# Issuing a pairwise-product kernel's stores and later loads from GpSimd's queue, one packet per DMA engine and transfer

## The chip, the core and the metric

The kernel runs on one core of a Trainium2 chip. The metric is the device time of one execution in microseconds. Before the change three runs took 1284.17, 1285.41 and 1285.61 us; their median, 1285.41 us, is what the changed kernel is compared with.

## What is computed

```python
def _L0_rec_ref(x, W):                      # x [4096, 32, 64] f32, W [64, 64] f32
    vid = jnp.einsum('bfd,de->bfe', x, W)
    idx_i, idx_j = jnp.triu_indices(32, k=1)
    return x[:, idx_i, :] * vid[:, idx_j, :]      # [4096, 496, 64]
```

Each of 4096 rows holds 32 fields of 64 numbers. Every field is multiplied by one 64x64 matrix, and then, for each of the 496 pairs i < j, field i is multiplied number by number with the transformed field j. The input is 33.6 MB and the output 520.1 MB, so nearly all that moves between the core and its memory is output.

## The kernel before

The host lays the batch out so that partitions hold (half of the batch, number within the field): two halves of 64 numbers make 128 partitions. A *tile* is 128 batch rows of each half; there are 16 tiles. In SBUF there is one large tensor, `mem`, of 445 *units*; a unit is 128 numbers, 512 bytes, in each of the 128 partitions. A tile of input takes 32 units (one for a field); a pair's product takes one unit, so 16 x 496 = 7936 units of output go out.

**Inputs** lie at the top of `mem` in two groups, `GROUPS`: tiles 0 to 7, and from tile 8 on the other eight. Tile 0 comes by itself in two transfers of the smaller tensor `x0`. The rest of group 0 comes in three pieces (128, 70 and 26 units), and group 1 in three more (102, 128 and 26 units), which overwrite group 0 when it is used up. `load(g)` issues a group.

**TensorE** multiplies each tile by a 128x128 matrix `w2` that holds W twice on its diagonal, and leaves the result in PSUM (`vid`), half a tile at a time, in a loop of its own.

**VectorE** (DVE) makes the products: 270 `tensor_tensor` instructions on line 299, each of which reads one operand from `mem` and one from `vid` and writes to `mem`. All its work stands in program order.

**Stores.** The stream of 7936 product units is cut into 74 *slots* (`SLOTS`: length, home in `mem`, and places where an instruction is split). As soon as the last product of a slot is issued, `store(slot, last)` issues one DMA of that slot, `(p u) c -> p u c`: each partition writes one contiguous row of up to 128 units, 64 KB, to the output. Homes are reused all the time: a product that is written over an old slot waits for that slot's store. Everything runs in the order in which it is written; no scheduler reorders anything.

**Queues.** A `Queue` object remembers what its engine already knows, so that it waits only for what it does not know. `transfer` (line 194) allocates a semaphore `moved<n>`, issues the DMA and adds 16 to the semaphore on landing. Loads go out on SyncE's queue (SP). Stores go out on SP up to slot 45, and from slot 46 (`SECOND`) on ScalarE's queue (ACT). GpSimd (POOL) has only four small memsets at the start. Each queue is in order: an instruction that waits holds what stands behind it. The first store after each group's loads also waits for that group's second piece (`hold[-2]`). At the end SP waits for what has not been heard of (line 313).

The constructor of the program sets aside 512 bytes in each partition for descriptors that software writes (`dynamic_dma_scratch_size=512`); before the change nothing used them.

Of the kernel before, what the change touches and what calls it, by code (L numbers as in the profile page):

```python
# [38 lines left out]
]  # L39

SECOND = 46


PAD = 24
# [111 lines left out]
def place_of(t, fields):  # L158

    first = max(begin for begin, _ in GROUPS if begin <= t)  # L160
    return TOP - (t - first + 1) * fields


def ends(tiles):
    return [begin for begin, _ in GROUPS[1:]] + [tiles]


def overlap(a, b):
    return a[0] < b[1] and b[0] < a[1]


def pairwise_bilinear_kernel(nc, x0, x, out):
# [8 lines left out]
    mem = ctx.enter_context(nc.sbuf_tensor([P, UNITS, C], F32))  # L181
# [5 lines left out]
    there = nc.alloc_semaphore("there")  # L187

    behind = {}
    sp, act, dve = (Queue(engine, behind) for engine in (nc.sync, nc.scalar, nc.vector))  # L190
    moved = []
    worked = []

    def transfer(out_, in_, units, reads, needs, queue=sp):
        sem = nc.alloc_semaphore(f"moved{len(moved)}")
        queue.issue(lambda: queue.engine.dma_start(out=out_, in_=in_), needs).then_inc(sem, 16)  # L196
        queue.note(sem, 16)
        moved.append((units, reads, sem))
        return sem

    def after(units):

        needs = [(s, 16) for u, reads, s in moved if reads and overlap(u, units)]
        last = max((n for spans, n in worked if any(overlap(units, s) for s in spans)), default=0)
        return needs + [(made, last)] * (last > 0)
# [3 lines left out]
    def work(make, spans, needs, tells):  # L209
# [8 lines left out]
    place = place_of(0, F)  # L218
    first = [
        transfer(  # L220
            mem[:, :, :].rearrange("p u c -> p (u c)")[:, (place + HALF) * C : (place + F) * C + D],
            x0.rearrange("p u c -> p (u c)")[:, HALF * C : F * C + D],
            (place + HALF, place + F + 1), False, [],
        ),
        transfer(mem[:, place : place + HALF, :], x0[:, :HALF, :], (place, place + HALF), False, []),
    ]
    work(lambda: nc.vector.memset(w2[:, :], 0.0), [], [], made)  # L227
# [11 lines left out]
    def load(g):  # L239
        (begin, pieces), end = GROUPS[g], ends(NT)[g]  # L240
        begin = max(begin, 1)
        low = place_of(end - 1, F)
        sems = []
        for lo, hi in pieces:
            at = (begin - 1) * F + lo - low
            sems.append(transfer(mem[:, lo:hi, :], x[:, at : at + hi - lo, :], (lo, hi), False, after((lo, hi))))
            loads.append((range(begin, end), (lo, hi), sems[-1]))
        return sems

    def loaded(t):  # L250
        units = (place_of(t, F), place_of(t, F) + F)
        return [(sem, 16) for tiles, piece, sem in loads if t in tiles and overlap(piece, units)]

    hold = load(0)
    begins = [begin for begin, _ in GROUPS]
    held = []

    def store(slot, last):
        nonlocal hold
        begin, end = STARTS[slot : slot + 2]  # L260
        home = SLOTS[slot][1]
        units = (home, home + end - begin)
        needs = [(made, last)]
        if hold:
            needs.append((hold[-2], 16))
            hold = []
        rows = out[BLOCKS[slot] : BLOCKS[slot + 1], :].rearrange("(p u) c -> p u c", p=P)
        transfer(rows[:, : end - begin, :], mem[:, units[0] : units[1], :], units, True, needs, act if slot >= SECOND else sp)


    for t in range(NT):
        if t in begins[1:]:
            hold = load(begins.index(t))
            for late in held:
                store(*late)
            held = []
        xs = (place_of(t, F), place_of(t, F) + F)
        blocks = list(products(by_block(), t * NP))
        for k, (at, n, nest, i, j) in enumerate(blocks):
            slot = bisect_right(STARTS, at) - 1  # L280
            begin, end = STARTS[slot], STARTS[slot + 1]
            home = SLOTS[slot][1]
            units = (home + at - begin, home + at - begin + n)
# [11 lines left out]
            needs = [(there, 2 * t + 2 - high), *after(units)]  # L295
# [9 lines left out]
            if at == end:  # L305
                late = (slot, counts[made])
                group = sum(behind <= slot for behind in STRETCHES)
                if t < begins[group]:
                    held.append(late)
                else:  # L310
                    store(*late)
# [65 lines left out]
```

## Time and profile before

| what | value |
|---|---|
| runs | 1284.17, 1285.41, 1285.61 us; median 1285.41 |
| span of the profiled execution (first to last instruction) | 1282.6 us |
| median of the runs less that span | 2.8 us |
| DVE busy | 1079.9 us, 84% |
| TensorE matmuls | 179.4 us, 14% |
| transfers | 8 loads and 74 stores, 553.70 MB |

The page gives for the profiled execution its span alone, from the first instruction to the last. The median of the runs is 2.8 us longer than that span, and lies around it in launch and end. Sums below are made in the span and then set against the median by the same 2.8 us.

How to read the profile: a row of the chain of waits or of the timeline has the start in microseconds, the duration, the engine and line, and the names of what is written and read. A chain row "DMA out_dram<-mem" runs from the issue of a store to the moment its semaphore tells that it has landed. The table of DMA issues has the transfer's size in KB for each group of equal issues and the median time from issue to landing; the size is left out where a row of a partition is exactly 64 KB (8192 KB in all). "SPq" and "ACTq" are the queues of SyncE and ScalarE. The view by windows has the share of time that the 16 DMA engines were busy, and GB/s, as its last two numbers.

### The profile page before, as it was taken

To read this page: it belongs to the slowest core of one execution; us is meant where nothing else is said; L and a number is where in the kernel's file an instruction comes from. 1 tells how busy PE (TensorE), PEld (TensorE's weight loads), DVE (VectorE), ACT (ScalarE), POOL (GpSimd) and SP (SyncE) were. 2 spreads that over 40 slices of the span, in tenths; PEclk is the share of its full clock that TensorE was granted. 3 is DMA by queue.
4 is the path that set the end of the run, shared out by engine and by line. 5 is a ranking of instruction groups with operands and counts; after the bars stand their busy time and mean duration, and the time that the engine had idled before them with its cause. 6 is when DMAs were issued, how large, how long until landed. Compare 5 with 4: busy or idle time off the path is not lost. (4 is left out here: it accounts for less than half of the span.)

```text
span 1282.6 us, 1255 instructions
## 1 busy us (share of the span) xinstructions
PE 179.4 (14%) x256; PEld 70.2 (5%) x256; DVE 1079.9 (84%) x273; POOL 0.2 (0%) x4
## 2 busy tenths in 40 slices
PE   2011120301111030300020111103020020201100
PEld 1000000100000010100010000001010010100000
DVE  6589989988897989998027989989988899899980
POOL 0000000000000000000000000000000000000000
PEclk8566565756656565655565655656556575656555
DMA  9999999999999999999999999999999999999999
GB/s 404 423 435 435 438 433 433 439 435 425 435 444 429 425 437 442 428 425 446 416 426 437 426 433 436 438 434 434 439 431 442 421 437 435 427 446 429 434 425 409
DMA packets 11810, 553.70 MB, mean 432 GB/s; under 512 B 1312, under 2 KB 1312, under 8 KB 1312
## 3 DMA queue, kind: packets, MB, share of 16 engines
q1 hardware_dynamic: 7776, 340.30, 61.5%
q10 hardware_dynamic: 4032, 213.39, 38.4%
q14 instruction: 2, 0.02, 0.0%
HBM read 33.59 MB, written 520.09 MB: 432 GB/s over the span
## 5 line engine op out<-in xcount | busy, mean ns | idle before, releaser
L299 DVE TENSOR_TENSOR mem<-mem,vid 128x1024 f32<-128x1024 f32 (+11 forms) x270 | 1079.3, 4065 | 161.2 <-DMA out_dram<-mem 114.5
L319 PE MATMUL vid<-mem,w 128*128 x256 | 179.4, 866 | 1016.1 <-PEq L317 1016.1
L319 PEld LDWEIGHTS vid<-mem,w 128*128 128x128 f32 x256 | 70.2, 288 | 1124.4 <-issue 1124.4
L230 DVE COPY w<-mem 64x64 f32<-64x64 f32 x2 | 0.4, 191 | 5.1 <-DMA mem<-in_r_x_dram 5.0
L227 DVE MEMSET w<- 128x128 f32 x1 | 0.2, 165 | 0.8 <-PEq L344 0.8
L344 POOL MEMSET const-bfloat16-1.0<- 128x1 bf16 x1 | 0.1, 101 | 0.0
L344 POOL MEMSET const-uint8-127<- 128x1 uint8 x1 | 0.1, 101 | 0.0
L344 POOL MEMSET const-float32-0.0<- 128x1 f32 x1 | 0.1, 98 | 0.2 <-issue 0.2
L344 POOL MEMSET const-float32-1.0<- 128x1 f32 x1 | 0.1, 98 | 0.0
## 6 DMA issues: line engine op xcount, KB each, us to landing
out_dram<-mem ACTq DMA_DIRECT2D x9, 7680.0 KB, 23.3
out_dram<-mem SPq DMA_DIRECT2D x4, 6656.0 KB, 20.5
out_dram<-mem SPq DMA_DIRECT2D x3, 7680.0 KB, 23.1
out_dram<-mem ACTq DMA_DIRECT2D x3, 7168.0 KB, 21.5
out_dram<-mem SPq DMA_DIRECT2D x5, 4096.0 KB, 17.5
out_dram<-mem SPq DMA_DIRECT2D x3, 5632.0 KB, 18.4
out_dram<-mem SPq DMA_DIRECT2D x3, 5120.0 KB, 17.3
out_dram<-mem SPq DMA_DIRECT2D x2, 7168.0 KB, 22.6
```

Source lines behind the costliest of these rows:

```text
L227: work(lambda: nc.vector.memset(w2[:, :], 0.0), [], [], made)
L230: lambda: nc.vector.tensor_copy(w2[half, half], mem[half, place + F, :D]),
L299: lambda: nc.vector.tensor_tensor(o, left, right, ALU.mult),
L319: last = nc.tensor.matmul(vid[:, b : b + BANK, :], lhsT=w2[:, :], rhs=xt(b), start=True, stop=True)
L344: nc = _bacc.Bacc("TRN2", target_bir_lowering=False, num_devices=1, dynamic_dma_scratch_size=512)
```

## The change

The change replaces the ACT queue by one on GpSimd (`pool`), and moves to it every store and the three loads of group 1. The two loads of `x0` and the three of group 0 stay on SP. A DMA from GpSimd's queue has its descriptors written by software, into the 512 bytes per partition named above. [...] Sizes, homes, waits and the order of transfers stay as they are.

```diff
-SECOND = 46
...
-    sp, act, dve = (Queue(engine, behind) for engine in (nc.sync, nc.scalar, nc.vector))
+    sp, pool, dve = (Queue(engine, behind) for engine in (nc.sync, nc.gpsimd, nc.vector))
...
     def transfer(out_, in_, units, reads, needs, queue=sp):
         sem = nc.alloc_semaphore(f"moved{len(moved)}")
-        queue.issue(lambda: queue.engine.dma_start(out=out_, in_=in_), needs).then_inc(sem, 16)
+        packet = {"single_packet": True} if queue is pool else {}
+        queue.issue(lambda: queue.engine.dma_start(out=out_, in_=in_, **packet), needs).then_inc(sem, 16)
...
-            sems.append(transfer(mem[:, lo:hi, :], x[:, at : at + hi - lo, :], (lo, hi), False, after((lo, hi))))
+            queue = pool if g else sp
+            sems.append(transfer(mem[:, lo:hi, :], x[:, at : at + hi - lo, :], (lo, hi), False, after((lo, hi)), queue))
...
-        transfer(rows[:, : end - begin, :], mem[:, units[0] : units[1], :], units, True, needs, act if slot >= SECOND else sp)
+        transfer(rows[:, : end - begin, :], mem[:, units[0] : units[1], :], units, True, needs, pool)
```

**At the head, SP's queue before.** The rows name the line, the DMA with what it writes and reads, partitions x numbers, and in brackets the semaphores it waits for (`made` counts DVE's instructions, `moved3` is the landing of group 0's second piece):

```order
L196 DMA mem<-in_r_x_dram 128x2112 [waits barrier_Pool_Activation_PE_DVE_SP_release]
L196 DMA mem<-in_r_x_dram 128x2048
L196 DMA mem<-in_r_x_dram 128x16384
L196 DMA mem<-in_r_x_dram 128x8960
L196 DMA mem<-in_r_x_dram 128x3328
L196 DMA out_dram<-mem 128x10240 [waits moved3,made]
L196 DMA out_dram<-mem 128x13952 [waits made]
```

Of these, SP keeps the five loads. The first stores now stand on POOL's queue, behind its memsets:

```order
L342 MEMSET const-float32-0.0 128x1
L342 MEMSET const-float32-1.0 128x1
L342 MEMSET const-bfloat16-1.0 128x1
L342 MEMSET const-uint8-127 128x1
L193 DMA out_dram<-mem 128x10240 [waits barrier_Pool_Activation_PE_DVE_SP_gather,moved3,made]
L193 DMA out_dram<-mem 128x13952 [waits made]
```

So the first store, which waits for `moved3`, no longer stands behind the third piece of group 0 in one queue: the two are now in two queues.

**At the change of groups, POOL's queue now.** Here `moved39` and `moved40` are stores whose homes group 1's first piece overwrites, and `moved43` is the landing of its second piece:

```order
L193 DMA out_dram<-mem 128x16384 [waits made] x6
L193 DMA mem<-in_r_x_dram 128x13056 [waits moved40,moved39]
L193 DMA mem<-in_r_x_dram 128x16384
L193 DMA mem<-in_r_x_dram 128x3328 [waits made]
L193 DMA out_dram<-mem 128x13312 [waits moved43,made]
L193 DMA out_dram<-mem 128x10880 [waits made]
```

The same six rows stood in the same order, with the same waits, on SP's queue before; they have changed the queue and nothing else.

## The prediction

> **What bounds the kernel now.** I read the page first, then its stages by windows, then the queues, and last the chain of waits.
>
> ```profile
> span 1282.6 us, 1255 instructions
> ...
> PE 179.4 (14%) x256; PEld 70.2 (5%) x256; DVE 1079.9 (84%) x273; POOL 0.2 (0%) x4
> ...
> DMA packets 11810, 553.70 MB, mean 432 GB/s; under 512 B 1312, under 2 KB 1312, under 8 KB 1312
> ...
> q1 hardware_dynamic: 7776, 340.30, 61.5%
> q10 hardware_dynamic: 4032, 213.39, 38.4%
> q14 instruction: 2, 0.02, 0.0%
> ```
>
> DVE looks busy with 84%, but the two data queues together took 99.9% of what 16 DMA engines have. The DMA engines are the bound, and the packets tell how they work: 82 transfers of 128 rows are 10496 packets of one row each, and 82 x 16 = 1312 small ones, one per engine and transfer, that count the semaphore. By stage:
>
> ```profile
> 0.00:45.00 45.00, 8.59 (x16) 3.58 (x16) 28.55 (x12) 0.20 (x4) 0.72 0.98 409
> 45.00:600.00 555.00, 80.54 (x112) 31.29 (x112) 506.42 (x124) 0.00 (x0) 0.58 1.00 435
> 600.00:700.00 100.00, 8.65 (x16) 3.60 (x16) 34.00 (x13) 0.00 (x0) 0.55 0.99 423
> 700.00:1260.00 560.00, 81.62 (x112) 31.76 (x112) 510.90 (x126) 0.00 (x0) 0.57 1.00 434
> 1260.00:1283.00 23.00, 0.00 (x0) 0.00 (x0) 0.00 (x0) 0.00 (x0) 0.50 0.90 388
> ```
>
> In the two long stages of stores the share is 1.00. No engine has a gap that an earlier issue could fill. So the change can win only if a byte costs the DMA engines less, and lose only if it costs them more or opens gaps. DVE's waits are the consequence of this bound, not a second one:
>
> ```profile
> DVE mem L299 <- DMA out_dram<-mem: 114.5, 35, 18.3
> ```
>
> **The gain: what a packet costs.** Stores on the chain of waits give it, because start plus duration is the landing:
>
> ```profile
> 737.54 19.67 DMA out_dram<-mem
> ...
> 799.72 20.36 DMA out_dram<-mem
> ...
> 924.85 25.69 DMA out_dram<-mem
> ...
> 963.74 25.44 DMA out_dram<-mem
> ...
> 1085.24 27.13 DMA out_dram<-mem
> ...
> 1126.64 24.34 DMA out_dram<-mem
> ```
>
> Between the first two landings, 757.21 and 820.08, lie 62.87 us and five stores of 88, 72, 64, 85 and 107 units (the slots of the table at that place): 416 units, and 5 x 8 = 40 row packets on each engine. Between the next two, 950.54 and 989.18, lie 38.64 us and two stores of 128 units: 256 units, 16 packets. With u for a unit and c for a packet, its share of the small packet included: 416u + 40c = 62.87 and 256u + 16c = 38.64. Eliminating u leaves 14c = 62.87 - 62.79, so c is 6 ns. With the last two landings in place of the middle ones (38.61 us for the same sizes) it is 9 ns.
>
> 77 transfers move to POOL, 8 row packets on each engine: 616 packets. With one packet per engine and transfer, the most that can go is the whole of c: 616 x 6 ns = 3.7 us (5.5 us by 9 ns). The least is nothing, if c belongs to the row and not to the packet. The rows before cannot tell the two apart. I take a little over half of 3.7 us, **2.0 us**, since the packet's boundary and the row's own start both stand in c, and keep 0 and 5.5 for the range.
>
> [...] The trace agrees that c is small, 6 ns beside some 2.4 us for a 64 KB row (38.64 us over 16).
>
> **The issue path: what hides a slower one.** No row of before shows a software descriptor. The hardware path is bounded by the first load, which met an empty queue; the other rows show stores, that met a full one:
>
> ```profile
> mem<-in_r_x_dram SPq DMA_DIRECT2D x1, 1056.0 KB, 5.2
> ...
> out_dram<-mem ACTq DMA_DIRECT2D x9, 7680.0 KB, 23.3
> ...
> out_dram<-mem SPq DMA_DIRECT2D x15, 26.5
> out_dram<-mem ACTq DMA_DIRECT2D x11, 25.6
> ```
>
> A unit takes 38.64 / 256 = 0.151 us. The first load is 16.5 units, 2.5 us; of its 5.2 us, 2.7 us are start and landing. A store of 120 units (7680 KB) needs 18.1 of its 23.3 us, one of 128 units 19.3 of 25.6 or 26.5: 5 to 7 us remain. Subtracting the 2.7 us leaves about 2.5 to 4.5 us in which the transfer ahead still runs. The tightest store in the chain is the one at 737.54: 104 units, 15.7 us, 4.0 us remain, cover 1.3 us. So a software path up to 1.3 us longer than the hardware's costs nothing anywhere. If that cover is gone, each microsecond costs one at every such place. Between 0 and 2.5 us longer, I take **under 1.3 us, cost 0**: POOL has nothing else to do (0.2 us busy), each of its transfers waits for the same `made` count as before, and what is queued behind a waiting transfer is the next store in time, as it was. [...]
>
> **The head and the change of groups.** Loads before the first store stay on SP, and so does the start.
>
> ```profile
> 0.73 2.57 SPq L196 DMA_DIRECT2D mem<-in_r_x_dram  x5
> 38.45 0.82 SPq L196 DMA_DIRECT2D out_dram<-mem  x2
> ```
>
> and in the table of issues, for the first 5 us alone:
>
> ```profile
> mem<-in_r_x_dram SPq DMA_DIRECT2D x1, 1664.0 KB, 40.5
> ```
>
> The third piece of group 0 (1664 KB), issued as the fifth load within the first 3.3 us, lands at about 43; the first store is issued at 38.45, so 4.9 us of load cover POOL's first transfer. New is that the two now share the engines from two queues, the store in packets of a whole share (80 units, 12 us), the load row by row. The load may land tens of microseconds later. Its 26 units are fields of tile 7 alone, the last of the eight that use the first 622 us, so some 500 us hide it. At the change of groups the six rows keep their order. There the third load (1664 KB) covers the store behind it by its 26 units, 3.9 us. Both edits: 0.
>
> SP's queue loses 49 transfers and ACT's all 28; neither did anything else, and SP's wait at the end comes after the last landing in both. Cost 0.
>
> **Sum.** 1282.6 - 2.0 = 1280.6 us of span; with the 2.8 us around it **1283.4 us**, 0.16% below the median of the runs.
>
> **Rivals.**
>
> *Nothing merges* (the packet cost is the row's, or the flag does nothing): 1285.4. For it: c is so small that it may be the row's start. [...]
>
> *The software path is late* (slower). The price is at the stores that DVE's waits tie to the chain. Cover by the same subtraction, for all ten store rows of the chain, of which these stand between the quoted ones:
>
> ```profile
> 677.58 20.38 DMA out_dram<-mem
> ...
> 832.34 22.76 DMA out_dram<-mem
> ...
> 868.11 22.00 DMA out_dram<-mem
> ...
> 1002.18 23.22 DMA out_dram<-mem
> ```
>
> With 104, 104, 107, 120, 112, 128, 128, 120, 128 and 128 units, in order of time, the covers are 2.0, 1.3, 1.5, 2.0, 2.4, 3.7, 3.4, 2.4, 5.1 and 2.3 us. A path 2 us longer than the hardware's loses 1.2 us there, 2.5 us longer 3.6, 3 us longer 7.1. The chain covers the second half, so I double: 2.4, 7, 14 us, hence 1288, 1292.6 and 1300. It decides from 1.3 us on. Against it: that is nearly twice the hardware path's 2.7 us, landing included.
>
> [...]
>
> *DVE locks POOL out* (slower). If software could not write descriptors while a DVE instruction runs, each store would wait for the next one:
>
> ```profile
> L299 DVE TENSOR_TENSOR mem<-mem,vid 128x1024 f32<-128x1024 f32 (+11 forms) x270 | 1079.3, 4065 | 161.2 <-DMA out_dram<-mem 114.5
> ```
>
> 4.1 us on average, less 2.4 us of cover, at 74 stores: 126 us, 1411. [...] No run here shows it.
>
> *A long packet holds up program code.* The page's q14 row has two packets of instructions. They would now wait for up to 8 x 2.4 = 19.3 us; if DVE needed one at once, 1304. [...]
>
> **How the numbers follow.** A measurement here can tell about 0.2%, 2.6 us: "faster" is below 1282.8, "slower" above 1288.0. Forecast 0.52, spread from 1279.9 to 1285.4 with its weight about 1283: 0.27 faster, 0.25 same. Nothing merges 0.07, same. Late path 0.18: 0.17 slower, 0.01 same. Descriptors 0.13: 0.11 slower, 0.02 same. Lock-out 0.05 and code 0.05, slower. Together **0.27 faster, 0.35 same, 0.38 slower**. The range is **1280.2 to 1296.0**: from just inside the gain of 5.5 us to the dear ends of late path and descriptors; lock-out, code and the tails stay out, with less than 2 in 10. The forecast's own range is 1280.2 to 1285.4.
>
> **What would show it.** Right: a software queue with nearly all bytes, DMA share still 1.00 in the two long stages, DVE's waits for stores near 114.5 us, and, from landings as above, a smaller c. Merging shows if a packet is counted per engine and transfer. A late path shows as shares under 1.00 with issue-to-landing times above those of before; costly descriptors as full shares at lower GB/s; the lock as stores that start when a DVE instruction ends; code as a DVE gap of some 19 us that no semaphore ended. I am wrong if stores stay back to back and the time still rises, or if more than 5.5 us go.

## The result, and the profile after

The changed kernel takes 1290.86 us (median of four runs, 1290.64 to 1291.13) against 1284.79 us for the kernel before in the same job: 6.07 us more, a ratio of 1.0048 with a 95% interval of 1.0034 to 1.0062. The profiled execution took 1291.13 us, of which its span is 1289.8.

The page of the changed kernel, the lines that answer to those of before:

```profile
span 1289.8 us, 1255 instructions
...
PE 185.3 (14%) x256; PEld 71.6 (6%) x256; DVE 1079.9 (84%) x273; POOL 41.5 (3%) x81
...
DMA packets 11811, 553.71 MB, mean 429 GB/s; under 512 B 1312, under 2 KB 1312, under 8 KB 1312
...
q0 software_dynamic: 11088, 536.88, 96.7%
q1 hardware_dynamic: 720, 16.81, 3.1%
...
L193 POOL DMA_DIRECT2D out_dram<-mem x74 | 39.6, 536 | 1142.8 <-DVE mem L297 1104.0
```

Three things stand there. 536.88 MB went through a software queue, so the transfers took the way that the change says. The packets are as many as before, one for each row of a partition and one for each semaphore record: 77 x 144 = 11088, where one packet for each engine and transfer would be 77 x 16 = 1232. Whatever the flag `single_packet` does, a row is still a packet to the profiler. And GpSimd needs about half a microsecond for a transfer, 536 ns on average for a store.

By stage (the last two numbers are the share of time the DMA engines were busy, and GB/s):

```profile
0.00:45.00 45.00, 9.64 (x16) 3.90 (x16) 28.54 (x12) 1.39 (x6) 0.71 0.98 416
45.00:600.00 555.00, 83.61 (x112) 32.24 (x112) 504.37 (x124) 18.15 (x34) 0.57 1.00 432
600.00:700.00 100.00, 9.74 (x16) 3.91 (x16) 34.03 (x11) 3.24 (x6) 0.53 0.99 421
700.00:1260.00 560.00, 82.27 (x112) 31.60 (x112) 512.92 (x127) 18.69 (x35) 0.57 1.00 432
```

The share is 1.00 in both long stages, as before, but at 432 GB/s where it was 435 and 434. The engines have no gaps there; the same bytes keep them busy for longer. Counted from its issue, a store of the two commonest sizes lands no later: in the table of issues (size, median us to landing) the stores of 120 and of 128 units take 23.2 and 25.5 us, where 23.3 and 25.6 to 26.5 stood before. DVE's waits for stores come to 118.0 us for 114.5.

```profile
out_dram<-mem POOLq DMA_DIRECT2D x12, 7680.0 KB, 23.2
...
out_dram<-mem POOLq DMA_DIRECT2D x26, 25.5
```

```profile
DVE mem L297 <- DMA out_dram<-mem: 118.0, 35, 19.2
DVE mem L297 <- PE vid L317: 49.2, 2, 42.3
```

The chain of waits gives the same stores as before, so the landings can be set side by side:

```profile
682.07 18.59 DMA out_dram<-mem
...
740.23 0.39 issue
740.62 19.62 DMA out_dram<-mem
...
803.13 20.73 DMA out_dram<-mem
...
929.59 25.80 DMA out_dram<-mem
968.97 25.32 DMA out_dram<-mem
...
1133.01 24.29 DMA out_dram<-mem
```

The five stores between the landings at 760.24 and 823.86 take 63.62 us, 0.75 more than before; the two between 955.39 and 994.29 take 38.90, 0.26 more. From the first landing of this list to the last, 700.66 to 1157.30, lie 29 transfers and 456.64 us, against 453.02 before (697.96 to 1150.98): 3.62 us more. Not all of that is the price of a transfer, because an engine may already be at work on the next store when a landing is told: by the packet records of the next paragraph each engine moved 29 KB more in this stretch than before, about 1.1 us, and its rows took 2.46 us longer for the same bytes, 85 ns for each transfer.

One delay stands in the list too. The row before the store of 740.62 is 0.39 us of issue after the last product; before the change the same place showed 0.02 us:

```profile
737.52 0.02 issue
737.54 19.67 DMA out_dram<-mem
```

So the software path starts a store 0.37 us later. In the long stages the share of 1.00 shows no cost of it.

The trace also holds a record of each packet with its duration. Before the change, the median record of a row takes its size at 27.19 bytes per ns and 8 ns more; for 64 KB that is 2418 ns. What goes beyond that, as ns in each microsecond of transfer, was worked out from these records over all stores outside the change of groups, by the time since a store was issued:

```
time since the issue of a store       before   after
2 to 0.5 us earlier                     0.5      2.5
1.5 to 3.5 us later                     1.3     19.6
5.5 to 9 us later                       0.3      3.1
```

So there are two parts: a burst in the engines some 1 to 4 us after each issue, in the transfer that runs then, and a small surcharge all the time. The burst adds up to about 45 ns for a store, the surcharge (2.7 against 0.3 ns in each of some 16 us) to about 40. GpSimd's own instruction is over 0.53 us after the issue, before the burst begins. It is not a matter of a few engines: 2.5 us after an issue, all of the 16 rows in flight are over 5 ns too long at 37 of 67 stores, and at least 14 of them at 58; before the change no store shows this.

Added up over the whole run, the records come to 1287.4 us an engine, where they came to 1282.1: 5.3 us more. The two profiled executions lie 7.2 us apart, more than the medians do. The rest is idle time of the engines: about 1.0 us more at the change of groups (600 to 700 us) and 0.6 us more after 1240 us.

### The profile page after: what moved, and what is told of

The parts are those of the page before. It is cut to its first block, busy times and chain, and to the rows that moved or that the text cites. A ratio compares the mean times of both kernels' runs of the same rounds, so it can differ in the third digit from the quotient of the medians.

```text
span 1289.8 us, 1255 instructions
## 1 busy us (share of the span) xinstructions
PE 185.3 (14%) x256; PEld 71.6 (6%) x256; DVE 1079.9 (84%) x273; POOL 41.5 (3%) x81
## 3 DMA queue, kind: packets, MB, share of 16 engines
q0 software_dynamic: 11088, 536.88, 96.7%
## 5 line engine op out<-in xcount | busy, mean ns | idle before, releaser
L297 DVE TENSOR_TENSOR mem<-mem,vid 128x1024 f32<-128x1024 f32 (+11 forms) x270 | 1079.3, 4065 | 167.4 <-DMA out_dram<-mem 118.0
L317 PE MATMUL vid<-mem,w 128*128 x256 | 185.3, 891 | 1016.2 <-PEq L315 1016.2
L193 POOL DMA_DIRECT2D out_dram<-mem x74 | 39.6, 536 | 1142.8 <-DVE mem L297 1104.0
## 6 DMA issues: line engine op xcount, KB each, us to landing
out_dram<-mem POOLq DMA_DIRECT2D x12, 7680.0 KB, 23.2
```

The costliest lines, as they stand in the source:

```text
L297: lambda: nc.vector.tensor_tensor(o, left, right, ALU.mult),
L317: last = nc.tensor.matmul(vid[:, b : b + BANK, :], lhsT=w2[:, :], rhs=xt(b), start=True, stop=True)
```

## The experiments

Each run was timed in five rounds beside the kernel before on the same chip. "Theory D" in the expectations is that the engines pay for software descriptors.

**1. The flag alone.** Software descriptors without `single_packet`:

```diff
-        packet = {"single_packet": True} if queue is pool else {}
+        packet = {}
```

> The changed kernel without the one-packet flag: software descriptors alone. Theory D (the engines pay for software descriptors: about 0.08 us for each of 77 transfers, a few ns on every row and some 45 ns more in the row that runs while the next transfer is issued): 1290 to 1292, as the changed kernel; the flag neither saves nor costs. Rival P (the one long packet costs): back at 1285 to 1287, within 2 us of before. Rival M (the flag saves its 2 to 4 us, and the software path costs 8 to 10): 1293 to 1295.

Measured: 1290.64 us, ratio to before 1.0048 (1.0034 to 1.0062), the ratio of the changed kernel. The packets are the same in number:

```profile
DMA packets 11811, 553.71 MB, mean 429 GB/s; under 512 B 1312, under 2 KB 1312, under 8 KB 1312
...
q0 software_dynamic: 11088, 536.88, 96.8%
```

With rows of 13 to 64 KB the flag neither saves nor costs that can be measured; the loss belongs to the software path.

**2. A part of the stores.** Only the last 28 stores on the software queue; the edit is against the changed kernel:

```diff
+SECOND = 46
...
-            queue = pool if g else sp
+            queue = sp
...
-        transfer(..., units, True, needs, pool)
+        transfer(..., units, True, needs, pool if slot >= SECOND else sp)
```

> Software queue for the last 28 stores alone (those that were on ScalarE's queue); everything else as before. Theory D: 28/77 of 6.1 us, 2.2 us more than before: about 1287.0. Rival G (the loss sits at the head or at the change of groups, where queues and loads meet): 1285, no more than 0.5 us over before.

Measured: 1286.36 against 1284.64, 1.7 us more; ratio 1.0014 (1.0005 to 1.0023). By stage:

```profile
45.00:600.00 555.00, 84.71 (x112) 32.53 (x112) 506.48 (x124) 0.00 (x0) 0.56 1.00 435
700.00:1260.00 560.00, 86.69 (x112) 33.30 (x112) 510.57 (x126) 15.13 (x28) 0.55 1.00 433
```

The first stage, all hardware, keeps its 435 GB/s; the second, where POOL issues 28 stores, falls to 433. The loss stands where the software transfers are, and needs none of them at the head or at the change of groups; it is 1.7 us, where 2.2 had been expected.

**3 and 4. Twice the rows.** Each row of a store in two descriptors, with hardware queues (3) and with software and the flag (4, with 768 bytes for descriptors):

```diff
-        queue.issue(lambda: queue.engine.dma_start(out=out_, in_=in_), needs).then_inc(sem, 16)
+        parts = {"max_dma_last_dim": (units[1] - units[0]) * C * 2} if reads else {}
+        queue.issue(lambda: queue.engine.dma_start(out=out_, in_=in_, **parts), needs).then_inc(sem, 16)
```

This is the edit of run 3; run 4 adds the same `**parts` to the changed kernel's line. The packet of 17 that run 4's expectation speaks of would be 16 half rows and the record of the semaphore.

> The kernel before, but each partition's row of a store moves as two descriptors of half the size: 592 more rows on each engine, hardware queues. If the 6 ns found between landings is a cost of the row: 592 x 6 ns = 3.6 us more, about 1288.4. If it is a cost of the transfer: 1285.

> The changed kernel with each row of a store as two descriptors, one packet of 17 for each engine and transfer; room for descriptors 768 bytes. Theory D, cost by descriptor: the 3.6 us of the halved rows in hardware, 592 x 5 ns for the rows and another 74 x 45 ns for twice the descriptors at the issue: 3.6 + 3.0 + 3.3 over 1290.9, about 1300.8. If the software's extra is by transfer or by byte: 1290.9 + 3.6 = 1294.5. If rows merge in a packet and only the packet costs: 1291.

Measured: 1291.74 (ratio 1.0058, 1.0044 to 1.0072) and 1298.98 (1.0114, 1.0098 to 1.0129). The packets of the two runs:

```profile
DMA packets 21282, 553.70 MB, mean 429 GB/s; under 512 B 1312, under 2 KB 1312, under 8 KB 1312
```

```profile
DMA packets 21283, 553.71 MB, mean 427 GB/s; under 512 B 1312, under 2 KB 1312, under 8 KB 1312
```

Both show all half rows as packets: 592 more on each engine for the 74 stores, so that no packet of 17 stands in the trace. In hardware they cost 7.1 us, 12 ns a row; 6 had been expected. In software they cost 8.1 us, 1290.86 to 1298.98 across the two jobs. So a row is not cheaper with the flag. And the software's extra is 7.2 us here beside 6.1 with half as many descriptors: theory D in the form "so much for each descriptor" had asked for 6.1 + 3.0 + 3.3 = 12.4 us between the two runs, and falls in that form. With the 7.1 us for the rows, a price by the transfer alone gives 1290.86 + 7.1 = 1297.96 us. Solved for both, the pairs give a fixed 62 ns for a transfer and 2 ns for a descriptor, but the 2 ns are not shown to differ from nothing: they rest on 1.2 us between two differences of medians, and by the packet records the software's extra is no larger with twice the rows (4.7 us an engine, 5.3 without).

**5 and 6. Twice the transfers.** The last 37 stores as two transfers of half the units each, on hardware (5) and on software (6, 768 bytes). The edit of run 6 stands below; run 5 has the queues of before in its last line:

```diff
-        transfer(rows[:, : end - begin, :], mem[:, units[0] : units[1], :], units, True, needs, pool)
+        middle = (end - begin) // 2
+        for low, high in ((0, middle), (middle, end - begin)) if slot >= 37 else ((0, end - begin),):
+            part = (home + low, home + high)
+            transfer(rows[:, low:high, :], mem[:, part[0] : part[1], :], part, True, needs, pool)
```

> The kernel before, but the last 37 stores go out as two transfers of half the units each, on the same hardware queues: 296 more rows and 37 more semaphore records on each engine. By the halved rows in hardware (7.1 us for 592 rows, 12 ns a row): 3.6 us more than before, about 1288.2. It is the control of the next run.

> The changed kernel with the last 37 stores as two transfers each; room for descriptors 768 bytes. Theory D, now by transfer (62 ns for each transfer and 2 ns for each descriptor, from the four runs before): the control plus 6.1 us for 77 software transfers plus 37 x 0.079 = 2.9 us: about 9.0 us over the control, 1297. Rival R (the software's extra goes by bytes or by rows moved, not by transfers): 6.1 to 6.7 us over the control, 1294.5.

Measured: 1288.06 (1.0030, 1.0019 to 1.0040) and 1297.42 (1.0101, 1.0085 to 1.0116). The difference is 9.4 us where the price by transfer gave 9.0 and the price by bytes or rows 6.1 to 6.7. The bytes and the number of rows are those of the control, run 5; only the path differs, and 114 transfers in place of 77 pay for it: 82 ns each, beside 79 ns each for the 77.

**7, 8 and 12. Software transfers that carry almost nothing.** All loads and stores stay on hardware. Beside each of the first 37 stores one transfer of 64 KB goes out, from `w2` to a scratch tensor, which adds work that the kernel doesn't need: on ACT's queue (7, whose edit stands below), on POOL's (8), and on POOL's with the flag (12). Where the expectation of run 8 names the flag, the kernel had none; run 12 has it.

```diff
+    side = nc.dram_tensor("side", (37, P, C), F32, kind="Internal").ap()
...
+        if slot < 37:
+            transfer(side[slot, :, :], w2[:, :], (UNITS, UNITS), True, [(made, last)], act)
```

> The kernel before, and beside each of the first 37 stores one more transfer of 128 rows of 512 bytes from w2 to a scratch tensor in DRAM, on ScalarE's hardware queue, which is idle then. 8 rows of some 27 ns and one record on each engine: 37 x 0.23 = 8 us more, about 1293. It is the control of the next run.

> As the run before, with these 37 small transfers on GpSimd's queue (software descriptors, no packet flag is needed: with the flag); all stores and loads stay on hardware queues. Theory D (a software transfer costs the engines 0.06 to 0.08 us whatever it carries): 2.2 to 2.9 us over the control. Rival R (the cost goes with the bytes that software-described transfers move; these move 2.4 MB of 553.7): within 0.5 us of the control.

> The 37 small software transfers beside hardware stores once more, now with the one-packet flag: the run of the same transfers before had been built without it, against what its expectation said, and its trace shows 592 data packets of 4 KB (8 rows of 512 bytes in one), where the hardware queue had 4736 of 512 bytes. Theory D (the flag changes nothing; software joins rows up to some 4 KB by itself): 592 packets again and 1296.7 within 0.6. Rival M (the flag joins more, the record as well): fewer small packets and up to 0.5 us less.

Measured: 1294.16 (1.0075, 1.0061 to 1.0089), 1296.69 (1.0096, 1.0081 to 1.0112) and 1296.84 (1.0101, 1.0084 to 1.0118). The packets of run 7, of run 8 and of run 12:

```profile
DMA packets 17139, 556.14 MB, mean 430 GB/s; under 512 B 1904, under 2 KB 6640, under 8 KB 6640
```

```profile
DMA packets 12995, 556.14 MB, mean 429 GB/s; under 512 B 1904, under 2 KB 1904, under 8 KB 2496
...
q0 software_dynamic: 1184, 2.43, 0.5%
```

```profile
DMA packets 12995, 556.14 MB, mean 429 GB/s; under 512 B 1904, under 2 KB 1904, under 8 KB 2496
...
q0 software_dynamic: 1184, 2.43, 0.5%
```

The 37 software transfers cost 2.5 us more than hardware ones, 68 ns each, although they hold 0.5% of the engines' time and their data went more cheaply: 592 packets of 4 KB, whose records last 173 ns, where the hardware had 4736 rows of 512 bytes, 27 ns each, 216 ns for eight. With these 43 ns the path costs up to about 110 ns a transfer here; less if the records of the small rows overlap in time, for in the stage of 45 to 600 us the records of run 7 add up to 557.05 us an engine, and those of before to 556.09. The price does not depend on the stores' bytes being described by software: the stores of run 8 are hardware's, and 1.5 to 3.5 us after an issue in the first 600 us their rows take 17.0 ns in a microsecond too long, where those of run 7 take 6.0. The flag again changes neither the packets nor the time.

**9, 10 and 11. What it is not.** GpSimd writes 8 KB of SBUF at each store's issue, transfers in hardware (9); all transfers on SP's one queue (10, `SECOND = 99`); the changed kernel with 768 bytes for descriptors in place of 512 (11). The three edits, one after the other:

```diff
+    side = ctx.enter_context(nc.sbuf_tensor([32, 64], F32))
...
+        pool.issue(lambda: nc.gpsimd.memset(side[:, :], 0.0), [(made, last), (wrote, slot)]).then_inc(wrote, 1)
```

```diff
-SECOND = 46
+SECOND = 99
```

```diff
-    nc = _bacc.Bacc("TRN2", target_bir_lowering=False, num_devices=1, dynamic_dma_scratch_size=512)
+    nc = _bacc.Bacc("TRN2", target_bir_lowering=False, num_devices=1, dynamic_dma_scratch_size=768)
```

> [...] Theory F (the engines pay when they take in and work through software descriptors, not GpSimd's writing): as before, within 0.5 us. Rival W (GpSimd's writes into SBUF hold up the engines' reads): 74 x 0.08, up to 6 us more, 1290.

> The kernel before with every transfer on SyncE's one hardware queue (the change of queue at slot 46 is taken out). Theory D: as before, within 1 us. Rival Q (one queue in place of two is what costs, the software has no part in it): 1289 to 1291.

> [...] Theory D: as the changed kernel, 1290.8 within 0.6. [...]

Measured: 1284.51 (1.0002, 0.9993 to 1.0011), 1284.36 (1.0001, 0.9992 to 1.0010) and 1290.83 (1.0051, 1.0037 to 1.0065), beside 1284.16. In run 9 the writes are there:

```profile
L271 POOL MEMSET side<- 32x64 f32 x74 | 10.4, 141 | 1236.7 <-DVE mem L302 1236.7
```

74 writes by GpSimd cost nothing that can be measured, one hardware queue is as good as two, and more room for descriptors does not help. Run 11 also clears runs 4 and 6 of the suspicion that their 768 bytes mattered.

The software's extra in one table, each beside a hardware run with the same stores (a median moves by about 0.5 us, so a price by 6 to 20 ns, the more the fewer transfers carry it):

| pair | software transfers | extra, us | for each, ns |
|---|---|---|---|
| changed kernel, before | 77 | 6.07 | 79 |
| last 28 stores, before | 28 | 1.72 | 61 |
| two descriptors a row, 4 and 3 | 77 | 7.24 | 94 |
| two transfers a store, 6 and 5 | 114 | 9.36 | 82 |
| 64 KB transfers, 8 and 7 | 37 | 2.53 | 68, with cheaper data |

By the packet records alone, the extra of the first four pairs is 5.3, 1.8, 4.7 and 6.2 us an engine: 69, 64, 61 and 54 ns for each transfer. So some 54 to 69 ns are longer packets, and the rest of the table's prices is idle time and the scatter of the runs.

No run points to a version that beats the kernel before: those without software transfers equal it or are slower.

## Why the prediction was wrong

**The bound** was right: the DMA engines are busy in the long stages before and after, so only the price of a byte or gaps could move the time.

Two terms of the sum failed: the gain of 2.0 us did not come, and the issue path, put at 0, cost the 6.07 us that the change loses.

**The gain** put 6 ns on each packet, and had the flag take away "a little over half of 3.7 us". Nothing goes: run 1 shows the time without the flag, and the count of packets shows that rows stay rows. The bound of nothing, which the prediction kept for its range, was the truth. The choice between the two ends rested on no row, as its text says. That nothing merges, which run 1 shows for rows of 13 to 64 KB, should have had more weight than 0.07. The 6 ns itself was read from differences of 0.08 us; the packet records give 8 ns a row, and adding rows costs 12 ns a row on the time.

**The issue path** is where the loss came from, and not by the wait that the prediction weighed. It asked only when a transfer starts. That question it answered rightly: a store is issued 0.37 us later, and where the engines were running empty, at the change of groups, the first packet of a software load came 1.37 us after its issue, against 1.03 us for the first hardware load, so the path is about 0.7 us longer and inside the cover of 1.3 us. What it left out of the sum is that a software transfer costs the engines work while another transfer runs: by the packet records 69 ns each and 5.3 us in all for the 77. That was left to the rival of costly descriptors.

**The head** held: its last load did not suffer from sharing the engines (39.7 us to landing, 40.5 before).

```profile
mem<-in_r_x_dram SPq DMA_DIRECT2D x1, 1664.0 KB, 39.7
```

**The change of groups** was nearly right. Its 0 asked whether the third load covers the store behind it, and not whether anything covers the third load. That load, issued at 677.74, finds the engines running out of work, and they stand idle for about 1.0 us more than before; in runs 1 and 11 it is 0.35 and 0.64 us, and in run 2, whose loads stay on SP, nothing.

**The rivals.** Costly descriptors, at 0.13, came nearest to what happened: full shares at lower GB/s, the sign that was named for them, came with 1.00 at 432 GB/s where 435 and 434 stood. But the upper end of the range, 1296.0 us, holds a price of descriptors that no run shows; in its place the runs showed 70 to 80 ns for a transfer. Runs 3 and 4 show that it hardly grows with the descriptors, and runs 5 to 8 that each transfer pays it.

What is shown is that rows take longer some 1 to 4 us after a software issue, even rows of hardware transfers, and that neither the flag, the number of queues, the room for descriptors nor GpSimd's plain writes of 8 KB make it. Why they do isn't shown. Nor is a burst the software's alone: in run 3, all hardware and with twice the rows, one of 12.6 ns in a microsecond stands in the same 1.5 to 3.5 us. The standing surcharge isn't the software's own either: 2 to 0.5 us before an issue it is 3.3 ns in a microsecond in run 3 and 2.1 in the first 600 us of run 7, both without software transfers, beside 2.5 in the changed kernel. The causes of both stay open.

The late path fell: from issue to landing the times are those of before, and the idle time at the change of groups, at most 1.0 us, is the one cost of lateness that shows; why the engines stood idle for 0.6 us more after 1240 us stays open. So did the lock-out by DVE, whose price was 126 us, and the delayed program code, which would have shown as a gap of DVE that no semaphore ended. Before its products DVE was idle for 167.4 us, and the waits for stores (118.0) and for PE's `vid` (49.2) make 167.2 of them. Nor does the lock show in GpSimd's own times: its instruction took 531 to 665 ns for a store, beside DVE instructions of 4065 ns on average.

**The sum.** 2.8 us were put around the span; after the change it is 1291.13 - 1289.8 = 1.3 us. The 2.8 compared the span of one execution with the median of others.

The forecast was 1283.4 us, a gain, and a loss came. The time lay in the range only because the bounds of the unknown costs were kept in it; the likeliest case had the wrong sign.

## What to carry to other kernels

Where the DMA engines are full, count what a path costs the engines for each transfer, and not only what it costs the issuing queue: software descriptors added about 80 ns per transfer here, which no wait in the profile shows, only a busy share of 1.00 at fewer GB/s (432 where 435 and 434 stood). Keep bulk transfers with long rows on hardware queues there; with rows of 13 to 64 KB the one-packet flag saved nothing. A cost that the profile bounds only from zero to something should not be split down the middle in the direction that one hopes for.

## What the runs showed of the hardware that was not expected

- Behind a full queue a software transfer takes no longer from issue to landing than a hardware one: 25.5 us for 8192 KB, 25.6 to 26.5 in hardware. Its issue stands 0.39 us after the last product, where the hardware's stood at 0.02; with the engines running empty, 1.37 us passed from issue to first packet, 1.03 in hardware.
- Halving the rows of the stores costs 12 ns a row even in hardware, twice what the landings gave for a packet; the packet records of run 3 show the same burst after an issue, 26 ns in a microsecond at its peak, where whole rows show 1.6.
- The software transfers of runs 8 and 12, without the flag and with it, moved eight rows of 512 bytes as one packet of 4 KB, in 173 ns for 216. So small rows were joined without the flag; the price of the transfer here, 68 ns with that data, was larger than the gain.
